# Relation sums kept per tile in a circular accumulator and projected per block of 512 nodes, with a group's one-hots made by two broadcast operations

## The chip, the cores and the metric

The kernel runs on one core of a Trainium2 chip. The metric is the device time of one launch in microseconds (us), as the median of repeated executions. A separate execution was recorded by the hardware profiler; the durations of single instructions come from it.

Engine names in the profile: PE is TensorE's matmul stream and PEld its weight loads, DVE is VectorE, ACT ScalarE, POOL GpSimd, SP SyncE. "L445" is line 445 of the kernel. The clock column of a profile, where there is one, is the clock granted to TensorE as a share of full speed.

## The reference

A graph with 12500 nodes of 128 features and 200000 edges, sorted by destination, goes through two relational convolutions, and the result is added to the input and normalized. The relation of an edge is the argmax over ten of its 42 attributes.

```python
def _rgcn_layer(x, src, dst, edge_type, w_rel, root, bias):
    N = x.shape[0]
    seg = dst * NUM_REL + edge_type
    xs = x[src]
    sums = jax.ops.segment_sum(xs, seg, num_segments=N * NUM_REL)
    cnt = jax.ops.segment_sum(jnp.ones(seg.shape, x.dtype), seg, num_segments=N * NUM_REL)
    mean = (sums / jnp.maximum(cnt, 1.0)[:, None]).reshape(N, NUM_REL, -1)
    return jnp.einsum('nrd,rdo->no', mean, w_rel) + x @ root + bias

edge_type = jnp.argmax(msg[:, NODE_EMB_DIM:-NODE_EMB_DIM], axis=1).astype(jnp.int32)
h = jax.nn.relu(_rgcn_layer(x, src, dst, edge_type, w_rel1, root1, b1))
y = _rgcn_layer(h, src, dst, edge_type, w_rel2, root2, b2)
return _layernorm(x + y, axis=-1)
```

All of it is f32. The destinations are sorted, so 128 neighbouring edges reach a narrow window of nodes.

## The kernel before

**Tiles and groups.** The edges are cut into 1563 tiles of 128. Sixteen tiles make a group; 97 such groups, one of eight tiles and one of three make the 99 groups of a layer. A tile's edges are taken to reach at most 12 consecutive nodes (`WN`), counted from its first node, so a pair (relation, node) is one of 10 x 12 = 120 keys (`KW`). If the data breaks this, a flag selects a slower general path at the end; with this data it is not entered.

**Per group** (`sums`, `project`, `add`):

1. POOL issues one indirect DMA for each tile (L445, `gather`), which brings the 128 source rows, 512 bytes each, into `g[:, j, :]`. `g` has three group buffers (`RING = 3`), so POOL can be up to three groups ahead of what frees them.
2. DVE makes a one-hot matrix for each tile, `oh[:, j, :]` (L461): 128 edges x 120 keys, equal to the edge's weight `wE` where the key `keyE` matches and 0 elsewhere. The weight is one over the count of edges with the same destination and relation. Two more operations make `at` (L465), which says where each of 96 rows, 8 tiles x 12 nodes, lies in a window of 160 nodes.
3. PE multiplies g by the one-hot (L468), sixteen times, into `zp`: per tile, the sum for each key, features on the partitions. `zp` has one buffer of four PSUM banks. Except in the last two groups the sums run from the last tile to the first, and the first of them waits for all gathers of the group.
4. ACT copies `zp` to `zs` (L482, four copies), sorted by relation.
5. PE projects: for each half of the group, ten matmuls with `w` of the ten relations (L494), accumulated in PSUM as `pp`; ACT copies it to `ms` (L500); PE multiplies `ms` by `at` (L510), which adds up rows of the same node.
6. DVE adds the 160 columns to `acc` (L516), features x all nodes, at the group's first node. That address is read from a table `bt` at run time, four at a time.

An f32 matmul shows up as two MATMUL rows in the profile, which I call two passes.

**Per block of 512 nodes** (29 blocks; the last ones have 128 and 84 nodes), once the groups that can reach it are done (`done_after`): `block_in` loads the rows of x (and in layer 1 of the hidden state from `hD` in DRAM) and transposes them on PE (L386), with an ACT copy to `fT` (L388). `block_rows` adds the bias to the accumulator on DVE (L395), clears it in layer 0 (L397), and on PE adds the root product (L400) and the transposed accumulator (L401). `hidden` applies the relu on ACT and stores to `hD`; `final` adds x, normalizes (L426 to L436) and stores the output.

**Once, spread over layer 0** in chunks of 128 tiles: `types` (the argmax, L266 to L271, and the keys) and `count` (equal keys within 40 neighbours, L341 to L350, which gives the weights). The first two chunks of types and the first of count run ahead of layer 0. Layer 1 starts its gathers from `hD` once layer 0 has stored all of it.

**Order.** The kernel is written in program order with the projection of one group after the sums of the next. The order on each engine is made by a scheduler at build time, and tile pools set the waits for buffers; a few instructions are pinned to program order (`keep_in_program_order`). Each engine executes its own list in order. All gathers stand in POOL's list; SP issues most of the other DMAs, ACT those of the weights and of `bt`.

Of the kernel before, what the change touches and what calls it, by code (L numbers as in the profile page):

```python
# [9 lines left out]
F32 = mybir.dt.float32  # L10
# [19 lines left out]
HR = HT * WN  # L30
SW = 160
# [4 lines left out]
YB = 512  # L36
W = 128
# [6 lines left out]
def rgcn_resnorm_kernel(ctx: ExitStack, tc: tile.TileContext, x, src, dst, attr, w_rel1, root1, b1,  # L44
# [26 lines left out]
    NPAD = N + SW  # L71
# [15 lines left out]
    assert C == P and E % GT == 0 and 0 < HALF < P and NT % CT and groups[-1][1] > 1  # L87
# [5 lines left out]
    ps_f = ctx.enter_context(tc.tile_pool(name="ps_f", bufs=2, space=PSUM))  # L93
    ps_c = ctx.enter_context(tc.tile_pool(name="ps_c", bufs=1, space=PSUM))

    hD = dram.tile([N, C], F32, name="hD")
    KD = dram.tile([1, L + NT * P + L], F32, name="KD")
# [8 lines left out]
    zpool = fast.enter_context(tc.tile_pool(name="zpool", bufs=2))  # L106
    spool = fast.enter_context(tc.tile_pool(name="spool", bufs=3))
    ps_z = fast.enter_context(tc.tile_pool(name="ps_z", bufs=1, space=PSUM))
    ps_o = fast.enter_context(tc.tile_pool(name="ps_o", bufs=1, space=PSUM))
# [47 lines left out]
    def sources(c):  # L157
# [9 lines left out]
    columns = const.tile([P, SW], F32, name="columns")  # L167
    nc.gpsimd.iota(columns, pattern=[[1, SW]], base=0, channel_multiplier=0,
                   allow_small_or_imprecise_dtypes=True)
    iota = columns[:, :W]  # L170
    pads = const.tile([P, L + 1], I32, name="pads")
    nc.gpsimd.iota(pads, pattern=[[1, L + 1]], base=FAR, channel_multiplier=0)

    rank = const.tile([G, 2 * HR], F32, name="rank")
    nc.gpsimd.memset(rank, 1.0)
    nc.gpsimd.affine_select(rank, rank, pattern=[[1, 2 * HR]], compare_op=ALU.is_ge, fill=0.0, base=0,
                            channel_multiplier=-WN)
    nc.gpsimd.affine_select(rank, rank, pattern=[[-1, 2 * HR]], compare_op=ALU.is_ge, fill=0.0, base=WN - 1,
                            channel_multiplier=WN)
    lead = const.tile([G, 2 * HR], F32, name="lead")  # L180
    nc.gpsimd.memset(lead, 1.0)
    nc.gpsimd.affine_select(lead, lead, pattern=[[0, 2 * HR]], compare_op=ALU.is_equal, fill=0.0, base=0,
                            channel_multiplier=1)
    which = const.tile([G, 1], F32, name="which")
    nc.gpsimd.iota(which, pattern=[[0, 1]], base=0, channel_multiplier=WN, allow_small_or_imprecise_dtypes=True)
    row = const.tile([HR, 1], F32, name="row")
    nc.gpsimd.iota(row, pattern=[[0, 1]], base=0, channel_multiplier=1, allow_small_or_imprecise_dtypes=True)
    lane = const.tile([P, P], F32, name="lane")
    nc.gpsimd.iota(lane, pattern=[[1, P]], base=0, channel_multiplier=P,
                   allow_small_or_imprecise_dtypes=True)  # L190
    riota = const.tile([P, NREL], F32, name="riota")
# [3 lines left out]
    iotaP = bank[:, :SW]  # L195
    riotaP = bank[:, SW:SW + NREL]
    topP = [bank[:, (3 + k) * P // 2:(4 + k) * P // 2] for k in range(2)]
    nc.vector.tensor_copy(iotaP, columns)
# [11 lines left out]
    within = const.tile([HR, 1], F32, name="within")  # L210
    pw = ps_f.tile([P, YB], F32, name="pf")
    nc.tensor.matmul(pw[:HR, 0:1], rank[:, :HR], which, start=True, stop=True)
    nc.vector.tensor_tensor(within, row, pw[:HR, 0:1], op=ALU.subtract)
    nc.vector.tensor_tensor(rank, rank, lead, op=ALU.subtract)
    fl = const.tile([P, 1], F32, name="fl")
    nc.vector.memset(fl, 0.0)
    acc = const.tile([P, NPAD], F32, name="acc")
    negs = const.tile([1, L], F32, name="negs")
# [5 lines left out]
    bt = keep.tile([1, NG], I32, name="bt")  # L224
    b8_i = keep.tile([G, NG], I32, name="b8_i")
    full = NT // G
    nc.vector.memset(b8_i[:, full:], 0)
    nc.scalar.dma_start(bt[:, :full + 1], bass.AP(dst.tensor, dst.offset, [[1, 1], [G * P, full + 1]]))
    nc.scalar.dma_start(b8_i[:, :full], bass.AP(dst.tensor, dst.offset, [[P, G], [G * P, full]]))
    for k, (t, n) in list(enumerate(groups))[full:]:  # L230
        if k > full:
            nc.scalar.dma_start(bt[:, k:k + 1], bass.AP(dst.tensor, dst.offset + t * P, [[1, 1], [1, 1]]))
        m = n if t + n < NT else n - 1
        nc.scalar.dma_start(b8_i[:m, k:k + 1], bass.AP(dst.tensor, dst.offset + t * P, [[P, m], [1, 1]]))
    nc.scalar.dma_start(b8_i[m:n, NG - 1:], bass.AP(dst.tensor, dst.offset + E - P, [[1, 1], [1, 1]]))
    b8 = keep.tile([G, NG], F32, name="b8")
    place = keep.tile([HR, 2, NG], F32, name="place")
    wide = const.tile([P, 1], F32, name="wide")
    nc.vector.memset(wide, 0.0)

    def places():
        early(0, nc.vector.tensor_scalar(bt, bt, 0, N - 1, op0=ALU.max, op1=ALU.min))
        early(0, nc.vector.tensor_copy(b8, b8_i))
        pw = ps_f.tile([P, YB], F32, name="pf")
        for h in range(2):
            nc.tensor.matmul(pw[:HR, h * NG:(h + 1) * NG], rank[:, h * HR:(h + 1) * HR], b8, start=True, stop=True)
        nc.vector.tensor_scalar(place, pw[:HR, :2 * NG].rearrange("p (h g) -> p h g", h=2), within, None, op0=ALU.add)
        nc.vector.tensor_reduce(wide[:HR], place, axis=AX.XY, op=ALU.max)
# [123 lines left out]

    def block_in(k, l):

        n0, n, subs = block(k)
        last = "e" if k == NBLK - 1 else ""
        b = len(subs) if last else 4
        xb = fin.tile([P, b, C], F32, name="xb" + last)
        rows_dma(xb, x, k, False)
        fb = xb  # L380
        if l:
            fb = fin.tile([P, b, C], F32, name="hb" + last)
            rows_dma(fb, hD, k, False)
        pt = ps_f.tile([P, YB], F32, name="pf")
        for t, h in subs:
            nc.tensor.transpose(pt[:, t * P:t * P + h], fb[:h, t, :], ident[:h, :h])  # L386
        fT = fin.tile([P, b * P], F32, name="fT" + last)
        nc.scalar.activation(fT[:, :n], pt[:, :n], AF.Copy)  # L388
        return xb, fT

    def block_rows(fT, k, l):

        n0, n, subs = block(k)
        a = fin.tile([P, YB], F32, name="a")
        nc.vector.tensor_scalar(a[:, :n], acc[:, n0:n0 + n], bsb[l], None, op0=ALU.add)  # L395
        if l == 0:
            nc.vector.memset(acc[:, n0:n0 + n], 0.0)  # L397
        pr = ps_f.tile([P, 4, C], F32, name="pf")
        for t, h in subs:
            nc.tensor.matmul(pr[:h, t, :], fT[:, t * P:t * P + h], rsb[l], start=True, stop=False)  # L400
            nc.tensor.matmul(pr[:h, t, :], a[:, t * P:t * P + h], ident, start=False, stop=True)  # L401
        return pr
# [5 lines left out]
    def hidden(k, ready):  # L408

        xb, fT = ready  # L410
        pr = block_rows(fT, k, 0)
        hb = fin.tile([P, 4, C], F32, name="hb")
        for p, s in spans(k):
            nc.scalar.activation(hb[:p, s], pr[:p, s], AF.Relu)
        rows_dma(hb, hD, k, True)

    def final(k, ready):

        xb, fT = ready
        pr = block_rows(fT, k, 1)  # L420
# [30 lines left out]
    def halves(n):  # L451
        return [(h, min(HT, n - h * HT)) for h in range(-(-n // HT))]
# [320 lines left out]
```

## Time and profile before

| what | value |
|---|---|
| median of three timed executions | 3974.79 us (3973.82 to 3981.2) |
| the profiled execution | 4772.34 us, of it the span from first to last instruction 4770.4 |
| granted TensorE clock, mean over the span | 0.739 |
| gathers | 3126, 944 ns each |
| first gather; last of layer 0 ends; first of layer 1; last ends | 4.30; 2390.5; 2422.18; 4732.4 us |

The profiled execution is 20% longer than the timed ones. A difference of this size means that its stalls can't simply be carried over; its durations of single instructions can.

Rows that stand around the change, as line, engine, operation, output<-inputs, count, then busy time, mean ns of one, and the idle time in front with what ended it:

```profile
L468 PE MATMUL zp<-oh,g 128*128 128x120 f32 x6252 | 1033.5, 325 | 293.5 <-issue 259.9
L482 ACT ACTIVATE zs<-zp 128x480 f32<-128x480 f32 (+1 forms) x782 | 382.9, 575 | 2167.7 <-remote 1912.9
L510 PE MATMUL pp<-at,ms 96*128 96x160 f32 (+1 forms) x784 | 198.1, 386 | 591.1 <-issue 405.0
L500 ACT ACTIVATE ms<-pp 96x256 f32<-96x256 f32 x196 | 74.1, 378 | 1241.3 <-remote 861.3
L465 DVE TENSOR_SCALAR at<-bank,place 96x160 f32<-96x160 f32 x392 | 131.9, 376 | 0.0
L426 DVE TENSOR_TENSOR v<-pf,xb 128x512 f32<-128x512 f32 (+1 forms) x28 | 17.4, 620 | 243.2 <-remote 238.3
```

"Issue" is time in which an engine waited for nothing that the profile shows; "remote" is a wait whose releaser could not be named.

### The profile page before, as it was taken

What the parts mean: (1) busy time and instruction counts of PE and PEld (TensorE: products, weight loads), DVE (VectorE), ACT (ScalarE), POOL (GpSimd) and SP (SyncE); (2) the same over time, 40 slices, a digit from 0 to 9 for tenths busy, and PEclk for the clock granted to TensorE, in tenths of its full rate; (3) what the DMA queues carried; (4) which work ended last, traced back from release to release, by engine and by line L of the source; (5) the groups of instructions that cost most, each with busy time, mean ns of one, the idle gap of its engine ahead of it and who ended that gap; (6) DMA issues with size and microseconds to landing.
All of it is one profiled execution on the core that took longest, in us unless ns stands there. A gap on an engine that the chain in (4) does not pass through costs nothing.

```text
span 4770.4 us, 43637 instructions
## 1 busy us (share of the span) xinstructions
PE 2759.5 (58%) x16162; PEld 2520.6 (53%) x16162; DVE 1511.5 (32%) x4652; ACT 527.0 (11%) x1136; POOL 2955.2 (62%) x3142
## 2 busy tenths in 40 slices
PE   2455556555655555666645555666655656565656
PEld 1455555555554545555544555555555555555556
DVE  5233333333333333333222222222222223222323
ACT  1011111111111101111110111111111111111111
POOL 5666665666656666666546666666666666666663
PEclk9677777777777777777776777777777777777778
DMA  4122122122221221212111211221222222222211
GB/s 141 44 79 74 50 74 74 50 75 62 61 77 47 75 62 51 57 48 52 46 49 46 54 52 51 53 56 51 52 56 53 52 52 58 51 52 52 58 52 40
DMA packets 180554, 279.00 MB, mean 58 GB/s; under 512 B 55623, under 2 KB 127190, under 8 KB 177206
## 3 DMA queue, kind: packets, MB, share of 16 engines
q0 software_dynamic: 100032, 205.07, 16.9%
q1 hardware_dynamic: 75428, 69.58, 4.6%
q8 instruction: 132, 2.16, 0.2%
q10 hardware_dynamic: 4872, 1.45, 0.1%
q14 instruction: 90, 0.74, 0.1%
HBM read 262.28 MB, written 13.60 MB: 58 GB/s over the span
## 4 chain that ended last, share of the span: by engine, by line
another core or an unknown queue 34%; PE 33%; issue 21%; DVE 11%; ACT 1%; DMA 0%; DVEq 0%; ACTq 0%; SPq 0%
PE pp L494 16%; PE zp L468 11%; DVE oh L461 7%; PE pp L510 2%; PE pf L401 1%; PE pf L400 1%; DVE at L465 1%; ACT zs L482 1%; DVE acc L516 1%; PE pf L343 0%; PE pf L345 0%; PE pf L386 0%; DVE o L436 0%; DVE st L429 0%
## 5 line engine op out<-in xcount | busy, mean ns | idle before, releaser
L445 POOL DMA_INDIRECT g<-in_x_dram,idxE x1563 | 1475.9, 944 | 911.2 <-issue 445.8
L445 POOL DMA_INDIRECT g<-hD,idxE x1563 | 1476.6, 945 | 865.3 <-issue 455.6
L494 PE MATMUL pp<-w,zs 128*96 128x128 f32 x7840 | 1358.2, 336 | 860.4 <-issue 722.1
L494 PEld LDWEIGHTS pp<-w,zs 128*96 128x96 f32 x7840 | 1232.0, 212 | 982.9 <-issue 834.6
L461 DVE TENSOR_SCALAR oh<-bank,keyE,wE 128x120 f32<-128x120 f32 x3126 | 1000.1, 400 | 644.6 <-remote 576.6
L468 PE MATMUL zp<-oh,g 128*128 128x120 f32 x6252 | 1033.5, 325 | 293.5 <-issue 259.9
L468 PEld LDWEIGHTS zp<-oh,g 128*128 128x128 f32 x6252 | 983.1, 240 | 314.0 <-issue 292.5
L482 ACT ACTIVATE zs<-zp 128x480 f32<-128x480 f32 (+1 forms) x782 | 382.9, 575 | 2167.7 <-remote 1912.9
L516 DVE TENSOR_TENSOR acc<-acc,pp 128x160 f32 x198 | 63.7, 322 | 1634.4 <-remote 1043.0
L510 PE MATMUL pp<-at,ms 96*128 96x160 f32 (+1 forms) x784 | 198.1, 386 | 591.1 <-issue 405.0
L510 PEld LDWEIGHTS pp<-at,ms 96*128 96x128 f32 (+1 forms) x784 | 142.5, 232 | 633.8 <-issue 437.1
L500 ACT ACTIVATE ms<-pp 96x256 f32<-96x256 f32 x196 | 74.1, 378 | 1241.3 <-remote 861.3
L341 DVE TENSOR_TENSOR eqb<-pf,kh 128x1344 bf16<-128x1344 f32 (+1 forms) x65 | 100.6, 1552 | 181.4 <-PE pf L345 82.3
L400 PE MATMUL pf<-root,fT 128*128 128x128 f32 x388 | 110.1, 379 | 79.0 <-issue 49.1
L401 PE MATMUL pf<-ident,a 128*128 128x128 f32 x392 | 114.0, 388 | 60.3 <-DVE a L395 22.0
L400 PEld LDWEIGHTS pf<-root,fT 128*128 128x128 f32 x388 | 87.0, 276 | 91.2 <-issue 55.8
L465 DVE TENSOR_SCALAR at<-bank,place 96x160 f32<-96x160 f32 x392 | 131.9, 376 | 0.0
L401 PEld LDWEIGHTS pf<-ident,a 128*128 128x128 f32 x392 | 90.7, 285 | 68.6 <-issue 24.6
L426 DVE TENSOR_TENSOR v<-pf,xb 128x512 f32<-128x512 f32 (+1 forms) x28 | 17.4, 620 | 243.2 <-remote 238.3
L348 DVE TENSOR_REDUCE wp<-pf 128x128 f32<-128x512 f32 (+1 forms) x13 | 9.0, 691 | 182.9 <-remote 175.5
L343 PE MATMUL pf<-eqb,identb 128*128 128x512 bf16 (+1 forms) x130 | 50.5, 388 | 17.9 <-DVE f L320 17.0
L388 ACT ACTIVATE fT<-pf 128x512 f32<-128x512 f32 (+1 forms) x56 | 30.2, 539 | 207.1 <-remote 151.3
(107 smaller groups left out, 483.0 us busy)
## 6 DMA issues: line engine op xcount, KB each, us to landing
m<-in_edge_attr_dram SPq DMA_DIRECT2D x24, 1344.0 KB
g<-in_x_dram,idxE POOLq DMA_INDIRECT x1563
g<-hD,idxE POOLq DMA_INDIRECT x1563
xb<-in_x_dram SPq DMA_DIRECT2D x46, 256.0 KB
hD<-hb SPq DMA_DIRECT2D x23, 256.0 KB
hb<-hD SPq DMA_DIRECT2D x23, 256.0 KB
out_dram<-o SPq DMA_DIRECT2D x23, 256.0 KB
w<-in_L_gnn_w_rel_dram ACTq DMA_DIRECT2D x2, 640.0 KB
```

What stands on the lines that cost most here:

```text
L341: nc.vector.tensor_tensor(eq[:p], kp[:p, None, :R].to_broadcast([p, DB, R]), ahead, op=ALU.is_equal)
L400: nc.tensor.matmul(pr[:h, t, :], fT[:, t * P:t * P + h], rsb[l], start=True, stop=False)
L401: nc.tensor.matmul(pr[:h, t, :], a[:, t * P:t * P + h], ident, start=False, stop=True)
L445: return g, [then("POOL", nc.gpsimd.indirect_dma_start(out=g[:, j, :], out_offset=None, in_=table, in_offset=bass.IndirectOffsetOnAxis(ap= ...
L461: then("DVE", nc.vector.tensor_scalar(oh[:, j, :], iotaP[:, :KW], keyE[:, t:t + 1], wE[:, t:t + 1], op0=ALU.is_equal, op1=ALU.mult))
L465: nc.vector.tensor_scalar(at[:, h, :], iotaP[:HR], place[:, h, k:k + 1], None, op0=ALU.is_equal)
L468: m = nc.tensor.matmul(zp[:, j // QB, j % QB * KW:(j % QB + 1) * KW], g[:, j, :], oh[:, j, :], start=True, stop=True)
L482: then("ACT", nc.scalar.activation(zs[:, :, b * QB:b * QB + m, :], zp[:, b, :m * KW].rearrange("c (j r n) -> c r j n", r=NREL, n=WN), AF.C ...
L494: nc.tensor.matmul(po[:m * WN, h], zs[:, r, h * HT:h * HT + m].rearrange("c j n -> c (j n)"), wsb[l][:, r, :], start=(r == 0), stop=(r == ...
L500: nc.scalar.activation(ms[:, :n // HT], po[:HR, :n // HT], AF.Copy)
L510: nc.tensor.matmul(pa, ms[:m * WN, h], at[:m * WN, h], start=(h == 0), stop=(h == len(parts) - 1))
L516: nc.vector.tensor_tensor(acc[:, s], acc[:, s], pa, op=ALU.add)
```

## The change

1. **Accumulators.** `acc` no longer holds projected features of all nodes. It is used as `circle`: features x 10 relations x (1024 + 12) nodes, a ring of nodes. For each tile, DVE adds the 10 x 12 sums of `zp` straight into `circle` at the tile's first node modulo 1024. So there are 16 additions at run-time addresses per group, with one load of 16 offsets, in place of one addition with a load for every four groups. An extra 12 columns at the end take what crosses the seam; every 1024 nodes they are added to the front and cleared.
2. **Projection.** `zs`, `project`, `ms`, `at` and the matmul with `at` are gone. Once per block, `projected` multiplies ten slices of `circle` by `w`, 512 columns at a time, on top of the root product, and ACT clears the slices. `zp` is now two tiles of eight, in two buffers, so a group's second half is still freed apart from its first.
3. **Block end.** ACT adds the bias and, in layer 0, applies the relu; PE transposes the result back. In layer 0 the untransposed result is stored as well (`hT`), and layer 1 loads it in place of the rows of `hD` and four transposes.
4. **One-hots.** Two operations per group over 128 x 16 x 120: equality of the column number with the key, both broadcast, and multiplication by the weight, which ACT has copied to PSUM.
5. **Set-up.** The tables for `at` are gone from POOL, PE and DVE. A table of every tile's first node replaces that of every group's: a DMA of 1562 single values, and on DVE seven operations on one row of 1563 (cast, difference from an even spread, two clamps, sum, modulo, and a check in `flagged`).

The core of the diff:

```diff
-        for j in range(n):
-            t = t0 + j
-            then("DVE", nc.vector.tensor_scalar(oh[:, j, :], iotaP[:, :KW], keyE[:, t:t + 1], wE[:, t:t + 1],
-                                                op0=ALU.is_equal, op1=ALU.mult))
-        at = spool.tile([HR, 2, SW], F32, name="at")
-        for h, _ in halves(n):
-            nc.vector.tensor_scalar(at[:, h, :], iotaP[:HR], place[:, h, k:k + 1], None, op0=ALU.is_equal)
-        zp = ps_z.tile([P, G // QB, YB], F32, name="zp")
+        wP = weightP[k % 3][:, :n]
+        then("ACT", nc.scalar.activation(wP, wE[:, t0:t0 + n], AF.Copy))
+        then("DVE", nc.vector.tensor_tensor(oh[:, :n], iotaP[:, None, :KW].to_broadcast([P, n, KW]),
+                                            keyE[:, t0:t0 + n, None].to_broadcast([P, n, KW]), op=ALU.is_equal))
+        nc.vector.tensor_tensor(oh[:, :n], oh[:, :n], wP[:, :, None].to_broadcast([P, n, KW]), op=ALU.mult)
+        zp = [ps_z.tile([P, HT // QB, YB], F32, name="zp") for _ in range(0, n, HT)]
...
+    def add(k, zp):
+
+        t0, n = groups[k]
+        lo, hi = bounds(t0, n)
+        lo, hi = (lo % RN, hi % RN) if lo // RN == hi // RN else (0, RN - 1)
+        offs = nc.values_load_multi_w_load_instructions(
+            bt_i[0:1, t0:t0 + n], engines=[DVE], min_val=lo, max_val=hi,
+            skip_runtime_bounds_check_because="clamped to these nodes on the chip")[1]
+        for j in range(n):
+            s = circle[:, :, ds(offs[j], WN)]
+            z = tile_sums(zp, j).rearrange("c (r n) -> c r n", n=WN)
+            nc.vector.tensor_tensor(s, s, z, op=ALU.add)
...
+    def projected(fT, k, l):
+
+        n0, n, subs = block(k)
+        po = ps_p.tile([P, YB], F32, name="pp")
+        nc.tensor.matmul(po[:, :n], rsb[l], fT[:, :n], start=True, stop=False)
+        o = n0 % RN
+        if not o and k:
+            nc.vector.tensor_tensor(circle[:, :, :WN], circle[:, :, :WN], circle[:, :, RN:], op=ALU.add)
+            nc.scalar.activation(circle[:, :, RN:], zero[:, None, :WN].to_broadcast([P, NREL, WN]), AF.Copy)
+        H = NREL // 2
+        for q in range(0, NREL, H):
+            for r in range(q, q + H):
+                nc.tensor.matmul(po[:, :n], wsb[l][:, r, :], circle[:, r, o:o + n], start=False, stop=(r == NREL - 1))
+            nc.scalar.activation(circle[:, q:q + H, o:o + n], zero[:, None, :n].to_broadcast([P, H, n]), AF.Copy)
+        return po
...
     def places():
-        early(0, nc.vector.tensor_scalar(bt, bt, 0, N - 1, op0=ALU.max, op1=ALU.min))
-        early(0, nc.vector.tensor_copy(b8, b8_i))
...
+        early(0, nc.vector.tensor_copy(bt, bt_i))
+        early(0, nc.vector.tensor_tensor(off, bt, even, op=ALU.subtract))
+        early(0, nc.vector.tensor_scalar(bt_i, off, float(OFF), -float(OFF), op0=ALU.min, op1=ALU.max))
+        early(0, nc.vector.tensor_tensor(bt_i, bt_i, even, op=ALU.add))
+        early(0, nc.vector.tensor_scalar(bt_i, bt_i, 0, N - 1, op0=ALU.max, op1=ALU.min))
+        early(0, nc.vector.tensor_scalar(bt_i, bt_i, RN - 1, None, op0=ALU.bitwise_and))
...
-        nc.vector.tensor_scalar(a[:, :n], acc[:, n0:n0 + n], bsb[l], None, op0=ALU.add)
...
+        nc.scalar.activation(a[:, :n], po[:, :n], AF.Identity if l else AF.Relu, bias=bsb[l])
         pr = ps_f.tile([P, 4, C], F32, name="pf")
         for t, h in subs:
-            nc.tensor.matmul(pr[:h, t, :], fT[:, t * P:t * P + h], rsb[l], start=True, stop=False)
-            nc.tensor.matmul(pr[:h, t, :], a[:, t * P:t * P + h], ident, start=False, stop=True)
+            nc.tensor.transpose(pr[:h, t, :], a[:, t * P:t * P + h], ident)
...
-        pr = block_rows(fT, k, 0)
+        n0, n, _ = block(k)
+        a, pr = block_rows(sums_of(fT, k, 0), k, 0)
+        then("SP", nc.sync.dma_start(hT[:, n0:n0 + n], a[:, :n]))
```

In the program that results, each of the 16 additions waits for the one before it; the second of a group's two one-hot operations stands between additions of an older group; the first eight sums of a group wait for the first eight additions of the group before, the last eight for the last eight.

## The prediction

> **What bounds the kernel now.** I read the share of busy time first, then the costliest groups, then the waits of POOL, then its timeline.
>
> ```profile
> PE 2759.5 (58%) x16162; PEld 2520.6 (53%) x16162; DVE 1511.5 (32%) x4652; ACT 527.0 (11%) x1136; POOL 2955.2 (62%) x3142
> L445 POOL DMA_INDIRECT g<-in_x_dram,idxE x1563 | 1475.9, 944 | 911.2 <-issue 445.8
> L445 POOL DMA_INDIRECT g<-hD,idxE x1563 | 1476.6, 945 | 865.3 <-issue 455.6
> L494 PE MATMUL pp<-w,zs 128*96 128x128 f32 x7840 | 1358.2, 336 | 860.4 <-issue 722.1
> L461 DVE TENSOR_SCALAR oh<-bank,keyE,wE 128x120 f32<-128x120 f32 x3126 | 1000.1, 400 | 644.6 <-remote 576.6
> L341 DVE TENSOR_TENSOR eqb<-pf,kh 128x1344 bf16<-128x1344 f32 (+1 forms) x65 | 100.6, 1552 | 181.4 <-PE pf L345 82.3
> L516 DVE TENSOR_TENSOR acc<-acc,pp 128x160 f32 x198 | 63.7, 322 | 1634.4 <-remote 1043.0
> ```
>
> No engine is full. POOL is the fullest, and nearly all of it is one instruction, the gather of 128 rows. Now what POOL waited for, and one group of it:
>
> ```profile
> POOL g L445 <- issue: 901.4, 2925, 5.1
> POOL g L445 <- remote: 456.6, 129, 8.1
> POOL g L445 <- PE zp L468: 383.2, 61, 28.5
> POOL g L445 <- DMA hD<-hb: 31.7, 1, 31.7
> ```
>
> ```profile
> 1420.64 0.94 POOL L445 DMA_INDIRECT g<-in_x_dram,idxE  x1 [0.30 <-issue]
> 1425.12 0.94 POOL L445 DMA_INDIRECT g<-in_x_dram,idxE  x1 [3.55 <-remote]
> 1426.37 0.94 POOL L445 DMA_INDIRECT g<-in_x_dram,idxE  x1 [0.30 <-issue]
> ...
> 1443.84 0.95 POOL L445 DMA_INDIRECT g<-in_x_dram,idxE  x1 [0.30 <-issue]
> 1448.40 0.94 POOL L445 DMA_INDIRECT g<-in_x_dram,idxE  x1 [3.61 <-PE zp L468]
> ```
>
> Inside a group gathers start every 1.249 us (1425.12, 1426.37). That is 0.94 of work and 0.30 of "issue", which recurs before nearly every gather, so it is part of the gather's price. A group of 16 takes 19.98 us. Then POOL waits some 3.6 us, because the ring of three group buffers is full and the sums of an older group (L468) are late. So the recorded execution is bound by PE, at about 23.3 us per group.
>
> The timed runs are not. The recorded execution took 4772.3 us, the timed ones 3974.8. I split the recorded span: first gather at 4.3; 3126 x 1.249 = 3904 of gathers; 825 of larger gaps, of which 28.2 lie in the head (63.2 to 92.7), 31.4 at the layer boundary and some 766 in the ring stalls of single groups; 38 after the last gather. Sum 4771. The timed median has room for 4 + 3904 and some 66 more. Head, boundary and tail as recorded are 98. But two of these hold PE's backlog:
>
> ```profile
> 4738.07 4.53 PE L494 MATMUL pp<-w,zs 128*96 128x128 f32 x40
> ...
> 4755.11 0.60 PE L468 MATMUL zp<-oh,g 128*128 128x120 f32 x4
> ```
>
> The last gather ended at 4732.4, yet the last sums ran at 4755.1, behind the projections of older groups. At the boundary the distance is the same, 22.4 us (2390.5 to 2412.9). Without a backlog it would be about 6, so 16 go twice: 98 - 32 = 66. Hence the timed kernel is **bound by POOL issuing gathers**, with next to no ring stalls. The "issue" gaps of 1 to 2 us between single matmuls belong to the recording. What the change can move in the timed runs is head, boundary and tail (66 us), unless it makes another engine need more than 20 us per group.
>
> **The change part by part.**
>
> *PE.* Gone per group: the 40 passes of L494, four of L510. Per block come a root matmul and ten w·circle matmuls of 512 columns. The trace has no f32 matmul of this width; its 512-column bf16 pass takes 0.215 warm and 0.427 cold, so 11 x 2 passes are about 5 to 10 us each block if a pass is alike, doubled if an f32 pass takes two of those; I take 10. PE falls from 13 to 15 us busy per group to about 4 to 7, plus 10 per four groups. In the timed runs this is worth nothing: gathers hide it. In a recorded run it removes the 766.
>
> *DVE one-hots.* Sixteen of L461 start 0.31 apart (5.05 us) and two of L465 take 0.7. In their place stand two operations over 1920 elements. Nearest row: L341, 1344 elements in 1.552; scaled by element 2.15 each, 4.3 together. The ends are 1.9 and 2.5 each. Saving 1.4 per group, hidden.
>
> *DVE adds.* One L516 (0.32) becomes 16 dynamic adds of 120 elements, each waiting for the one before it, with a register operation each and one load of 16 offsets. L516 has 160 elements, so 0.28 to 0.32; a dependent operation starts 0.04 after its predecessor ends; the register operation (0.069) runs beside the predecessor in L516's rows. Spacing 0.32 to 0.36: 5.1 to 5.8 us, plus 0.4 to 0.8 for the load (a load of four takes 0.34, on a busy engine 0.79). Upper end: the register operation and its wait don't overlap, 0.5 each, 8 us. I take 5.3 + 0.6: no row shows a reason for the gap.
>
> *The new wait.* Two halves of PSUM hold one group: the first eight sums of group k+1 wait for adds 0 to 7 of k, the last eight for adds 8 to 15. Behind the waiting matmul stand all later PE work, and for its end wait the adds of k+1 and the gathers of k+4. Chain per group: DVE 4.3 + 5.9 = 10.2, the sums' second half 1.8, hops 0.3: **12.3 us, against 19.98 for the gathers**.
>
> Here a rule speaks against the change. The Trainium skill, "TensorE: Matmul & The Clock Gate", Part 1 (HAM clock gate): after an idle window of about 3.4 us TensorE falls to half its clock and needs as long busy to recover. A PE with 5 us of work in 20 would then be cold most of the time. The trace has both speeds: a pass of L468 takes 0.112 warm, 0.213 cold, and the granted clock is 0.739 on average. By the warm row the second half (16 passes) is 1.8, by the rule 3.4, so the chain is 12.3 or 13.9; the block's matmuls take up to 18 instead of 10. Both stay below the cover: four groups have 80 us, and even 4 x 13.9, 8 more of projection between two sums, 7 of DVE at a block of layer 1 (L426 to L436) come to 71. In layer 0 the types and count steps add about 9 of DVE per four groups (five L341 per eight groups make half of it): 73. The ring holds more than 30 us of lag for uneven groups. Cost 0; if the cover goes, the excess over 80 is paid 50 times.
>
> *ACT.* Four zs copies and ms (2.3 us per group) go; weight copy, zeroing (two of 2560 elements, about 2.4 each from the 512-column fill of 0.61), a and hb come. A weight copy may queue behind a zeroing that waits for the projection, so one-hots can be some 6 us late once a block. Hidden by the ring.
>
> *POOL, SP, DMA.* POOL loses about 1.4 us of head set-up that stands behind the first gathers. SP gets one store of hT per block of layer 0 ahead of hD's, and one load in place of hb's in layer 1; both far ahead of use, except at the boundary (below). Gathers beside L395 averaged 0.974 against 0.944; L395 goes: 58 x 0.03 = -2 us.
>
> *Head.* Seven operations on one row of 1563 come before the first argmax: 1.0 to 1.8 each, 9 to 12 us; about 5 of it falls where DVE waited for a DMA (14.9 to 20.3). That is +4 to +7 on the chain to the first weights, wE at 80.5, and so on the 28.2 us for which POOL stands. Given back: the first L341 now follows two small operations instead of some ten slow self-waiting ones (57 to 66.9), up to -10; one-hots -0.7. From -7 to +8; I take 0, since both lie on the same chain.
>
> *Boundary and tail.* The last sums to the first gather of layer 1 took 9.25 (2412.93 to 2422.18). Gone: 20 passes of L494 (2.1), ms, L510 and one add (1.4). Come: three adds (1.0), the last block's 11 matmuls of 84 columns (2 to 2.5), zeroing before it (1.4), bias, transpose instead of L400/L401 (+0.5), hT's store ahead of hD's. +1.5 +-3, twice: +3.
>
> Sum: 0 - 2 + 0 + 3 = +1. On the recorded execution: 4772 - 766 - 32 of backlog + 1 = 3975; on the median of the timed runs, 3975 + 1 = **3976 us**. Its own range, from head and boundary, is 3962 to 3990. A measurement here tells 0.2% (8 us) from no change.
>
> **The rivals.**
>
> *DVE becomes the bound (slower; 0.17).* Place: adds in layer 0. Price: the upper end above, 0.5 an add instead of 0.33, adds 2.7 per group, so with a cold TensorE four groups take 73 + 11 = 84 in layer 0 and 82 in layer 1 against 80: 25 x 4 + 25 x 2 = 150 more, 4126. It decides from about 0.44 per add (7 us spread over 64 adds). For it: self-waiting small operations in the head show gaps of 1.3 to 2.6 us. Against: those have "issue" and "remote" as their cause, and operations of 0.82 in the argmax start 0.86 apart.
>
> *Before was held by more than gathers (faster; 0.20).* If the gather is cheaper unrecorded than 1.249, before was partly bound by PE, and the change frees it: at 1.22, 3126 x 0.029 = 91 less, 3885; or only some 15 us of ring stalls remain in the timed runs, 3960. For it: the split of 66 us rests on my estimate of the backlog. Against: the sum closes at 1.249 within 2 us.
>
> *Head decides (slower; 0.08).* Nothing of the +8 is given back and the boundary takes +6 more: 3990.
>
> *Nothing hidden changes (0.55)*, the forecast: of it 0.25 within 0.2%, 0.16 faster by the head's gain, 0.14 slower.
>
> Together: faster 0.36, same 0.25, slower 0.39. The range for 8 in 10 takes in part of both tails: 3915 to 4060.
>
> **What would show it.** In the changed kernel's profile: a span near 3975, gathers 1.249 apart through whole groups with few gaps above 0.30; 16 adds in 5 to 6 us; the two one-hot operations near 2.15; PE under 35% busy with a low granted clock; POOL's stall in the head between 20 and 36. Wrong if POOL waits in most groups for sums, and those for adds, or if the gap between gathers itself differs.

## The result, and the profile after

The changed kernel takes **3992.68 us** (median of five executions, 3991.27 to 3994.05). Five executions of the kernel before, taken beside it, have a median of 3973.87 (3973.28 to 3981.2). The ratio is 1.0047 with a 95% interval of 1.0036 to 1.0057: the change makes the kernel 18.8 us slower, a small loss that is clear of the noise.

In every recording of the kernel before and in all experiment runs each kernel took some 16 to 20% longer than in the runs above, because PE's matmuls or its signals came late (the last section), so those runs are compared only among themselves. The recording of the changed kernel is free of this: it is one of the five executions, with a time of 3992.68, a span of 3990.8 and a mean clock of 0.704.

First the rows of the page of the changed kernel that answer to those shown of before: busy time and share of each engine, then groups of instructions with busy time, mean ns of one, and idle time in front.

```profile
PE 1771.3 (44%) x8122; PEld 1419.5 (36%) x8122; DVE 1946.0 (49%) x4394; ACT 357.8 (9%) x523; POOL 2957.3 (74%) x3136
L451 POOL DMA_INDIRECT g<-in_x_dram,idxE x1563 | 1479.5, 947 | 496.5 <-issue 469.0
L451 POOL DMA_INDIRECT g<-hD,idxE x1563 | 1475.2, 944 | 501.5 <-issue 471.5
L495 DVE TENSOR_TENSOR acc<-acc,zp 128x120 f32 x3126 | 863.8, 276 | 1506.8 <-PE zp L472 1371.7
L386 PE MATMUL pp<-acc,w 128*128 128x512 f32 (+2 forms) x1160 | 437.0, 533 | 11.7 <-DVE acc L495 7.0
L467 DVE TENSOR_TENSOR oh<-bank,keyE 128x1920 f32<-128x1920 f32 (+1 forms) x198 | 419.8, 2120 | 25.9 <-PE zp L472 25.0
L469 DVE TENSOR_TENSOR oh<-oh,bank 128x1920 f32<-128x1920 f32 (+1 forms) x198 | 419.6, 2119 | 0.2
```

The engine that gained work is DVE (32% before, 49% now). It waits 1372 us for sums, so it is not short of time. POOL's waits say the same from the other side (total, number, longest):

```profile
POOL g L451 <- issue: 940.5, 3086, 0.3
POOL g L451 <- DMA hD<-hb: 25.4, 1, 25.4
POOL g L451 <- PE zp L472: 20.1, 3, 17.5
```

The "issue" gaps are never longer than 0.3: gathers start 1.250 us apart, group after group, and of 3125 gaps only four are larger. They are 17.5 us in the head, 1.7, 0.9, and 25.4 at the layer boundary. So the ring never runs full in mid-layer. The span is 4.5 to the first gather, 3126 gathers at 1.250 (3907), 44 more for the four gaps, and 35 after the last gather. So the changed kernel can have lost 18.8 us in three places only: head, boundary and tail.

### The profile page after: what moved, and what is told of

Same layout as the page of the kernel before. It is cut to its first block, busy times and chain, and to the rows that moved or that the text cites. A ratio compares the mean times of both kernels' runs of the same rounds, so it can differ in the third digit from the quotient of the medians.

```text
span 3990.8 us, 29921 instructions
## 1 busy us (share of the span) xinstructions
PE 1771.3 (44%) x8122; PEld 1419.5 (36%) x8122; DVE 1946.0 (49%) x4394; ACT 357.8 (9%) x523; POOL 2957.3 (74%) x3136
## 5 line engine op out<-in xcount | busy, mean ns | idle before, releaser
L472 PE MATMUL zp<-oh,g 128*128 128x120 f32 x6252 | 1178.8, 373 | 2004.4 <-DMA g<-hD,idxE 996.7
L472 PEld LDWEIGHTS zp<-oh,g 128*128 128x128 f32 x6252 | 1143.1, 286 | 2099.9 <-issue 2081.0
L495 DVE TENSOR_TENSOR acc<-acc,zp 128x120 f32 x3126 | 863.8, 276 | 1506.8 <-PE zp L472 1371.7
L386 PE MATMUL pp<-acc,w 128*128 128x512 f32 (+2 forms) x1160 | 437.0, 533 | 11.7 <-DVE acc L495 7.0
L467 DVE TENSOR_TENSOR oh<-bank,keyE 128x1920 f32<-128x1920 f32 (+1 forms) x198 | 419.8, 2120 | 25.9 <-PE zp L472 25.0
L469 DVE TENSOR_TENSOR oh<-oh,bank 128x1920 f32<-128x1920 f32 (+1 forms) x198 | 419.6, 2119 | 0.2
L387 ACT ACTIVATE acc<-zero 128x2560 f32<-128x2560 f32 (+2 forms) x116 | 231.9, 2000 | 939.2 <-PE pp L386 939.2
L386 PEld LDWEIGHTS pp<-acc,w 128*128 128x128 f32 x1160 | 203.9, 196 | 210.6 <-issue 198.0
L405 PE MATMUL pf<-ident,a 128*128 128x128 f32 x196 | 34.7, 297 | 16.4 <-ACT a L402 16.3
L405 PEld LDWEIGHTS pf<-ident,a 128*128 128x128 f32 x196 | 26.3, 157 | 19.7 <-ACT a L402 19.7
```

The source lines that it names most:

```text
L386: nc.tensor.matmul(po[:, :n], wsb[l][:, r, :], circle[:, r, o:o + n], start=False, stop=(r == NREL - 1))
L387: nc.scalar.activation(circle[:, q:q + H, o:o + n], zero[:, None, :n].to_broadcast([P, H, n]), AF.Copy)
L405: nc.tensor.transpose(pr[:h, t, :], a[:, t * P:t * P + h], ident)
L467: then("DVE", nc.vector.tensor_tensor(oh[:, :n], iotaP[:, None, :KW].to_broadcast([P, n, KW]), keyE[:, t0:t0 + n, None].to_broadcast([P, n ...
L469: nc.vector.tensor_tensor(oh[:, :n], oh[:, :n], wP[:, :, None].to_broadcast([P, n, KW]), op=ALU.mult)
L472: m = nc.tensor.matmul(tile_sums(zp, j), g[:, j, :], oh[:, j, :], start=True, stop=True)
```

## Where the last groups wait

The timeline of PE in the tail of the changed kernel (start, duration, line, matmul, count, and idle time in front with what ended it). The last gather ended at 3955.85.

```profile
3949.48 2.40 PE L386 MATMUL pp<-acc,w 128*128 128x128 f32 x20
...
3958.14 4.05 PE L386 MATMUL pp<-acc,w 128*128 128x128 f32 x20 [4.62 <-DVE acc L495]
...
3967.90 4.48 PE L472 MATMUL zp<-oh,g 128*128 128x120 f32 x22 [4.08 <-DVE oh L469]
3974.21 3.87 PE L386 MATMUL pp<-acc,w 128*128 128x128 f32 x20 [1.83 <-DVE acc L495]
...
3980.06 2.46 PE L386 MATMUL pp<-acc,w 128*128 128x84 f32 x20 [0.38 <-DVE acc L495]
```

The sums of the last two groups (L472, 22 passes) start 12 us after the last gather. They wait for their one-hots, and DVE's timeline shows why these are late:

```profile
3964.29 0.18 DVE L436 BATCH_NORM_AGGREGATE mv<-st 128x2 f32<-128x6 f32 x1
3964.84 0.16 DVE L439 RECIPROCAL rstd<-rstd 128x1 f32<-128x1 f32 x1 [0.36 <-ACT rstd L438]
3965.04 0.34 DVE L442 TENSOR_SCALAR o<-v,mv,rstd 128x128 f32<-128x128 f32 x1
3965.45 1.16 DVE L467 TENSOR_TENSOR oh<-bank,keyE 128x960 f32<-128x960 f32 x1
...
3978.89 0.59 DVE L495 TENSOR_TENSOR acc<-acc,zp 128x120 f32 x2 [4.73 <-ACT acc L387]
```

The one-hots stand behind the normalization of a block, which waited for that block's projection. Later, the additions of the last three tiles (3978.89) wait 4.73 us for ACT to clear the slices (L387) of a block that is being projected. And two of the projections run cold: 20 passes of 128 columns took 2.40 at 3949.48, where the granted clock was 1.00, but 4.05 and 3.87 here, after PE had stood idle, where it was 0.59 and 0.61.

At the boundary PE shows the same chain. The last gather of layer 0 ended at 1979.2.

```profile
1979.60 2.50 PE L472 MATMUL zp<-oh,g 128*128 128x120 f32 x12
1986.80 4.63 PE L386 MATMUL pp<-acc,w 128*128 128x128 f32 x20 [4.69 <-DVE late L565]
1991.22 1.17 PE L472 MATMUL zp<-oh,g 128*128 128x120 f32 x6
```

The last sums (x6) run behind a projection, which is slow as well (4.63, at a granted clock of 0.50). That projection waited for additions: the one before it ended at 1986.74, just ahead of the operation on L565 that the row names. The trace of DVE has 4.3 us of one-hots (L467 at 1982.14, L469 at 1984.41) among these additions, and they are those of layer 1's first group, which nobody needs for another 40 us.

Of the kernel before there is no recording without the late signals, so its three places are known only in sum. Its time of 3973.87 is a span of about 3972.0. In the changed kernel everything from the 49th gather to the last, without the boundary, takes 3844.6. If before takes the same there, which means no ring stalls and the same spacing (none of its recordings can show it), that leaves 127.4 for the start of the 49th gather (the first after the stall in the head) plus boundary plus tail. In the changed kernel these are 85.8 + 25.4 + 35.0 = 146.2. The difference is the 18.8, by subtraction.

## The experiments

In each kernel the two ends after the last gathers were read: boundary (last gather of layer 0 to first of layer 1) and tail (last gather to the end). These stretches hold the backlog that a kernel brings along: in the changed kernel the two are 89.0 here and 60.4 in the undisturbed recording. So it is differences between kernels that are read, not the lengths. The runs were made on three chips; ratios are to the kernel before on the same chip, with 95% intervals.

```
kernel        time     ratio, interval            49th gather  ring stalls  boundary  tail
before_again  4768.64  (one run)                     92.3         756         31.7    38.0
before_3      4771.55  (one run)                     92.2         759         31.8    37.8
before_4      4767.78  (one run)                     91.6         748         31.7    38.0
after_again   4644.83  0.9763, 0.9741 to 0.9785      85.5         603         39.0    49.9
end_oh        4650.42  0.9759, 0.9745 to 0.9772      87.8         623         36.5    42.5
end_both      4645.98  0.9769, 0.9754 to 0.9783      87.7         613         34.3    42.0
ends          4639.06  0.9746, 0.9732 to 0.9759      87.4         626         33.0    37.2
ends_again    4639.94  0.9756, 0.9736 to 0.9775      88.0         625         33.0    35.8
ends_head     4653.22  0.9777, 0.9764 to 0.9791      91.5         630         33.1    35.8
places_late   4661.10  0.9787, 0.9773 to 0.98        95.6         626         39.2    51.3
oh_x2         4739.71  0.9950, 0.9935 to 0.9966      91.1         692         51.6    51.3
oh_single     4638.16  0.9756, 0.9737 to 0.9775      87.4         599         39.1    49.9
```

"Ring stalls" is the sum of POOL's gaps after the first 96 gathers beyond 0.3 each, without the boundary; they fall from some 755 to 603 with the change, which is most of why it is 2.4% faster in these runs and 0.5% slower where gathers run through.

**The two kernels again** (no edit).

> The unchanged kernel of before, profiled once more, to get an execution whose ring stalls are not those of the first recording. Theory A (the change loses at the two ends of a layer): if the recording is undisturbed (span near 3972), gathers stand 1.249 to 1.250 apart, POOL's stall in the head is 20 to 28 us, its wait at the layer boundary about 15 and the tail after the last gather 20 to 25, against 20, 25 and 35 in the changed kernel. Theory B (the head decides): head stall at most 5, boundary 25, tail 35. Theory C (gathers were cheaper before): spacing 1.244 or less.

> The changed kernel itself, beside before on the same chip. In the first four runs every kernel, before too, took about 4650 to 4770 us, and in their traces TensorE's signals reached the waiting engines only when POOL's gathers had stopped. If this chip does the same, I expect about 4660 against 4763 for before, a ratio near 0.98: one stop of some 2.6 us per group instead of 3.2 and more. If it does not, 3992 against 3974.

> The unchanged kernel of before, for a recording in which gathers run through. If it is one: theory A (the change loses at the ends of the layers): head stall 20 to 28 us, boundary wait about 15, tail 20 to 25, against 20, 25 and 35. Theory B (the head decides): head stall at most 5, boundary 25, tail 35. Theory C (gathers were cheaper before): spacing 1.244 or less.

> The unchanged kernel of before, for a recording in which gathers run through. Theory A: POOL stands at 80 to 92 us for its 49th gather; boundary wait plus tail 34 to 46, against 60 in the changed kernel. Where signals are held up: 92, and 70 for boundary and tail, as recorded twice.

None of the three recordings of before was undisturbed, so the values that theories A to C forecast for such a recording were not tested. The one line of POOL's waits that stands for the boundary, first of the kernel before (before_3), then of the changed kernel (after_again):

```profile
POOL g L445 <- DMA hD<-hb: 31.8, 1, 31.8
```

```profile
POOL g L451 <- DMA hD<-hb: 39.0, 1, 39.0
```

Boundary and tail together are 69.7, 69.6 and 69.7 in three recordings of before and 89.0 in the changed kernel: **19.3 us more, where 18.8 were lost**. The boundary has 4.0 more until the last sums end and 3.3 after them; the tail has 6.9 more until the last sums end and 5.1 after. Only the part until the last sums holds the backlog. In the changed kernel it is 26.5 and 30.2 here, against 13.2 and 16.5 undisturbed; what follows is 12.5 and 19.7, against 12.2 and 18.4. From the cold projection on, the tail repeats the waits of the undisturbed recording (PE of after_again):

```profile
4612.85 3.93 PE L386 MATMUL pp<-acc,w 128*128 128x128 f32 x20 [4.63 <-DVE acc L495]
...
4622.49 4.42 PE L472 MATMUL zp<-oh,g 128*128 128x120 f32 x22 [4.08 <-DVE oh L469]
4628.80 3.99 PE L386 MATMUL pp<-acc,w 128*128 128x128 f32 x20 [1.89 <-DVE acc L495]
...
4634.77 3.14 PE L386 MATMUL pp<-acc,w 128*128 128x84 f32 x20 [0.38 <-DVE acc L495]
```

So what comes after the last sums carries over to the timed runs of the changed kernel, and in before it takes 9.25 and 14.6. The 11 us until the last sums are a difference between two backlogs, and less sure for the timed runs.

**end_oh: the last two groups' one-hots ahead of the last additions.** They get tiles of their own and come before the blocks that end with those additions.

```diff
+            if k == NG - 2:
+                for e in (k, k + 1):
+                    early_oh[e] = one_hots(e)
             if end:
                 while held:
```

> The changed kernel, with the one-hots of the last two groups of a layer written ahead of the last full group's additions. Theory A: in the tail the sums of the group of eight no longer start at 3967.9 but as their gathers land, so the tail of 35.0 falls to about 25; the boundary, where these one-hots were early already, stays within 2 us: 3983 in all. Theories B and C: 3992, no change.

Boundary 36.5 and tail 42.5: 10 of the 19.3 are gone, 7.4 of them in the tail, where 10 were expected, and 2.5 at the boundary. The one-hots were late in the tail, as read above. The total didn't follow (ring stalls 623 against 603), so this run shows the place and not a gain.

**end_both: also, nothing of later use between the boundary's additions.** The first operations on the flag's tables go behind the last sums, and the first two one-hots of layer 1 behind layer 0's last addition.

```diff
+        if k < 2 and "add" in last:
+            tc.add_manual_dep(eq.ins, last["add"].ins.name, behind, reason="the last additions first")
...
+        for ins in first:
+            tc.add_manual_dep(ins.ins, last["sum"].ins.name, behind, reason="not at the boundary")
```

> The changed kernel with three things moved at the ends of the layers: the one-hots of the last two groups ahead of the last full group's additions, the first one-hots of layer 1 behind layer 0's last additions, and the flag's table work away from the boundary. Theory A, where gathers run through: tail 35.0 to about 25, boundary wait 25.4 to about 18, some 17 us in all: 3975, level with before. Theories B and C: 3992, no change. Where TensorE's signals are held up: about 10 us less than the changed kernel.

Boundary 34.3, another 2.2 less. That is half of the 4.3 us that the two one-hots take; the projection in front of the last sums stayed. The total did not fall by the 10 us that were expected: 4646 against 4645.

**ends, ends_again: also, the blocks that the last three groups complete wait for the last addition, and the last blocks of layer 1 are not cleared.** The clearing that is left out has no reader after it.

```diff
+        spent = l and done_after(k) > groups[NG - 3][0]
...
+            if spent:
+                continue
             nc.scalar.activation(circle[:, q:q + H, o:o + n], zero[:, None, :n].to_broadcast([P, H, n]), AF.Copy)
...
             add(k, zp)
+            if NG - 3 <= k < NG - 1:
+                return
```

> end_both, and the additions of the last three groups all ahead of the blocks that they complete: those three blocks are projected one after the other at the end, and layer 1 doesn't clear what it no longer reads. Theory A (the last groups' sums and the last blocks' projections stand in each other's way): tail of 42.0 in end_both to 33 or less, boundary wait of 34.3 to 30 or less, where TensorE's signals are held up; where gathers run through, tail 35.0 to about 22, boundary 25.4 to about 15, 3970 in all, below before. Rival (the ends are bound by what any order must do after the last gather): no more than 2 us.

> The kernel ends once more. Where gathers run through on this chip: 3970, against 3974 for before and 3992 for the changed kernel (theory A), or 3990 (the rival). Where signals are held up, 4639 as before, boundary and tail 33 and 37, which gives their scatter.

Boundary and tail come to 70.2 and 68.8, where before has 69.7. All of the 19.3 is taken back with the same sums, additions and projections: at the boundary by order alone (1.3 more than in before is left), in the tail by order and the clearings left out together (0.7 to 2.2 less than in before). Neither end came down to what was expected (a tail of 33 or less, a boundary of 30 or less). The tail of ends on PE, to be read against that of after_again (the last gather ended at 4611.6):

```profile
4619.23 2.40 PE L387 MATMUL pp<-acc,w 128*128 128x128 f32 x20
...
4625.43 5.02 PE L489 MATMUL zp<-oh,g 128*128 128x120 f32 x22 [2.16 <-DVE acc L513]
4630.24 3.03 PE L387 MATMUL pp<-acc,w 128*128 128x128 f32 x20
...
4635.07 2.50 PE L387 MATMUL pp<-acc,w 128*128 128x128 f32 x20 [0.73 <-DVE acc L513]
...
4638.43 2.40 PE L387 MATMUL pp<-acc,w 128*128 128x84 f32 x20
```

The idle times in front have shrunk, and with them the price of a projection after the last sums: 2.4 to 3.0 where it was 3.1 to 4.0. In the total time ends and ends_again are 5 to 6 us below the changed kernel, with intervals of the ratios that overlap, and their ring stalls are some 20 longer. So these runs don't show a faster kernel. Where gathers run through, 3992.7 less 19 to 20 would be about 3973, level with before; that is an estimate, and it was not measured.

**places_late and ends_head: the seven operations on one row of 1563 later.** In places_late they follow the first count (on the changed kernel), in ends_head they stand between types and count (on ends).

```diff
-    places()
     for _ in chain(types(0), types(1)):
         pass
     for _ in count(0):
         pass
+    places()
```

> The changed kernel, with the table of first nodes computed after the head's types and count. Theory A: wE some 5 us earlier, sums delayed by the two table operations that now stand beside the one-hots, POOL's head stall 17.6 to about 13: 3988. Theory B: most of the loss goes, 3978 or less.

> ends, with the table of first nodes computed between the types of the first two chunks and the first count, where the changed kernel's VectorE waits 5.7 us for a load. Theory A, by its steps (seven operations cost 4 to 7 us ahead of the first argmax): the keys of the second chunk at about 47 instead of 54, POOL's stall in the head 17 to about 12. Rival (places_late: the head is not bound by them): the stall stays at 17 or grows, because the small operations wait for each other as they did there.

Both missed: the 49th gather came later (95.6 and 91.5 against 85.5 and 87.4), not earlier. What the seven operations pushed back did come forward, the second chunk's first key (L289) from 54.1 in after_again to 45.2 in places_late. But then a chain of small operations fell in front of the count's first equality. DVE's timeline of places_late:

```profile
51.93 0.15 DVE L302 TENSOR_SCALAR f<-f 128x1 f32<-128x1 f32 x1 [1.80 <-remote]
54.03 0.29 DVE L300 TENSOR_REDUCE f<-bad 128x1 f32<-128x128 f32 x1 [1.95 <-remote]
...
57.53 0.16 DVE L304 TENSOR_TENSOR fl<-fl,f 128x1 f32<-128x1 f32 x1 [1.93 <-issue]
...
61.03 0.29 DVE L289 TENSOR_SCALAR key<-d_f 128x128 f32<-128x128 f32 x1 [3.18 <-issue]
```

Some operations of 0.15 to 0.3 us start 2 to 3.5 us after the one before, as they do in the recordings of before (57.05, 59.15, 61.95); in the changed kernel such operations stand 0.1 to 0.35 apart in both of its recordings (40.07 to 40.90 undisturbed). Why is open. So the runs say that the order in the head matters more than the seven operations, but not what the head of before costs where signals aren't late.

**oh_x2: two more equality operations per group**, which write the same values again, 4.3 us of DVE per group.

```diff
+        for _ in range(2):
+            nc.vector.tensor_tensor(oh[:, :n], iotaP[:, None, :KW].to_broadcast([P, n, KW]),
+                                    keyE[:, t0:t0 + n, None].to_broadcast([P, n, KW]), op=ALU.is_equal)
```

> The changed kernel, with two more equality operations over 1920 elements per group, 4.3 us more of DVE per group. Theory A, with a chain of 12.3 to 14 us per group under a cover of 19.98: gathers stay 1.25 apart in the middle of both layers; some 4 us more in the head and a few at the boundary: about 4000. Rival (DVE is already close to deciding): 2 us or more per group, over 4250.

It is 95 us slower than the changed kernel (89 by the ratios, as the two ran on different chips), some 0.48 per group for 4.3 of added work. If DVE were close to being the bound, each group would have paid 2 us and more. In the recordings 89 more are ring stalls and 13 more lie at the boundary. A group in these runs takes about 23 us and not 20, so the cover is larger here than in the timed runs; for those, what shows that DVE isn't the bound is the changed kernel's own trace (no ring stalls).

**oh_single: the changed kernel with the sixteen one-hots of before** and no copy of the weights.

```diff
+        for j in range(n):
+            t = t0 + j
+            then("DVE", nc.vector.tensor_scalar(oh[:, j, :], iotaP[:, :KW], keyE[:, t:t + 1], wE[:, t:t + 1],
+                                                op0=ALU.is_equal, op1=ALU.mult))
```

> The changed kernel with one part of the change undone: sixteen one-hot operations per group as before, and no weight copy. Theory A (the one-hots are hidden, 5.05 us on VectorE against 4.3, and the gain and the loss come from the projection's part alone): within 10 us of the changed kernel where signals are held up (about 4645 to 4655), a boundary and tail of 39 and 50 as in the changed kernel. Rival (the broadcast one-hots are what moves the time): back toward 4760 where signals are held up; toward 3974 where gathers run through.

Ends of 89.0, as in the changed kernel, and nearly the same time (4638 and 4645, ratios of 0.9756 and 0.9763 with intervals that overlap). The broadcast one-hots are no part of the loss.

## Why the prediction was right, and where it was not

Forecast 3976, measured 3992.7: inside the range of 3915 to 4060, just outside the likeliest case's own range of 3962 to 3990, and slower, to which 0.39 was given. The range was kept wide for the rivals; the sum itself gave +1 where +18.8 was measured.

- **The bound is POOL's gathers: right.** In the changed kernel no ring stalls are left, and head, boundary and tail are the only places that matter.
- **The recorded execution of before is bound by PE, and the change removes the 766: wrong in mechanism.** PE was held up there and stood still in 949 us of short pauses; its work was not the limit (the last section). With the change PE has 1771 us busy where it had 2760, or 1821 in after_again, and there 603 of some 755 us of ring stalls are still left.
- **PE's relief worth nothing in the timed runs: right, as far as the total shows.** PE is 44% busy, not under 35%. The block's ten matmuls of 512 columns take 8.76 (10 was taken for eleven), the sixteen sums 6.1: 8.3 per group of 20 us, which is inside the prediction's own terms; the 35% didn't follow from them.
- **Cold or warm PE: nearer to the rule.** In mid-layer the granted clock was 0.67 to 0.75 (four stretches of 80 us). The second half of the sums was put at 1.8 by the warm row and at 3.4 by the rule of the Trainium skill, "TensorE: Matmul & The Clock Gate", Part 1, that TensorE falls to half its clock after an idle window of about 3.4 us. Half of 6.1 is 3.05. In mid-layer this is hidden, as the prediction said. Its price at the ends was not in the sum.
- **DVE: right.** One-hots 2.15 each for a full group (2.15 predicted), additions 0.276 long and 0.313 apart (0.32 to 0.36). The load of sixteen offsets takes 1.10 instead of 0.4 to 0.8, off the chain.
- **The new wait hidden by the ring: right.** The gathers that reuse a buffer start 32 us after the sums that free it (at the least 23, behind the first groups).
- **Head 0: not refuted.** The stall is 17.5, below the 20 to 36 that the prediction looked for; the stall of before where signals aren't late isn't known. If the ends lost 19.3 in the timed runs as they did in the recordings, the head lost 18.8 - 19.3 = -0.5. That is argued from a difference; if the 49th gather of before started at 92.2 in the timed runs too, the head gained 6 and the ends lost 25. For the changed kernel it starts alike in both kinds of recording (85.8 and 85.5). How the 18.8 divide between head and ends stays open.
- **Boundary and tail: the step that failed.** The term was "+1.5 +-3, twice: +3"; the recordings give +7.3 and +12.0. It counted the instructions that the last block gains and loses, which stand behind the last sums: +3.3 and +5.1 there. For the time until the last sums it put nothing, and took for granted that they end about 6 us after the last gather, an estimate for before that no run measured. They ended 13.2 and 16.5 us after it. Left out were the one-hots standing behind a block's normalization, the block projection in front of the last sums, the wait of 4.73 for a clearing, and projections at the cold price of 3.9 to 4.6 instead of 2.4. Putting these into another order (end_oh, end_both, and ends, which also leaves out clearings) took back 10, 12.7 and 18.8 to 20.2 of the 19.3. Hence the cause is shown in the length of the ends in the recordings. No run shows it clear of noise in the total time, and that it accounts for the same 18.8 in the timed runs rests on the equal size.
- **Rivals.** DVE as the bound (4126) fell with the trace. Before held by more than gathers forecast a gain (3885 or 3960), and the changed kernel, which has no ring stalls at all, is not faster; a few us of ring stalls in the timed runs of before, made up for by a larger loss at the ends, are not excluded. Head decides (3990) has the number nearest to the measured one, but that is luck: the 49th gather starts at 85.8, not later than the 92 of before's recordings, and the tail, where most was lost, had no part in it. Only its boundary (1.5 and 6 more) came near the measured +7.3.

## What to carry to other kernels

Where one engine sets the pace throughout, price a change where this engine stands still: start, stage boundary, end. There the instructions of the last items come onto the path, and their order on the other engines counts as much as their number: list what stands in each queue behind the last transfer, at the price of an engine that has been idle. Work that moves from "per group" to "per block" leaves the hidden middle and returns, undivided, at each end.

## What the hardware showed besides

**Signals of PE that arrive late.** Gathers start 1.25 us apart while POOL runs. In the recording of the changed kernel 485 of 532 signals of PE (after the first 100 us) register within 1.25 us of a gather's start, so while POOL runs. In the run after_again only 71 of 500 do, and 323 register 3 to 5 us after the last gather's start, once POOL has stopped. One case in end_oh, POOL and PE:

```profile
1069.41 0.95 POOL L451 DMA_INDIRECT g<-in_x_dram,idxE  x1 [0.30 <-issue]
1073.08 0.95 POOL L451 DMA_INDIRECT g<-in_x_dram,idxE  x1 [2.73 <-PE pp L386]
```

```profile
1056.79 6.49 PE L482 MATMUL zp<-oh,g 128*128 128x120 f32 x32 [16.68 <-issue]
1063.12 8.76 PE L386 MATMUL pp<-acc,w 128*128 128x512 f32 x20
```

The sums ended at 1063.3 and the projection at 1071.9, yet signals of both registered together at 1072.82 to 1073.04. POOL and DVE waited for sums that had been done for 9 us. DVE's own signals in mid-layer were not held (additions 0.31 apart in both kinds of recording). What holds PE's stays open.

In the recordings of before PE's matmuls are held as well. PE and then POOL, in the first of them:

```profile
1005.85 0.26 PE L468 MATMUL zp<-oh,g 128*128 128x120 f32 x1 [1.82 <-issue]
1007.98 0.36 PE L468 MATMUL zp<-oh,g 128*128 128x120 f32 x1 [1.86 <-issue]
1010.08 0.36 PE L468 MATMUL zp<-oh,g 128*128 128x120 f32 x1 [1.74 <-issue]
...
1013.76 0.94 POOL L445 DMA_INDIRECT g<-in_x_dram,idxE  x1 [6.05 <-PE zp L468]
```

PE makes 619 such pauses of 1 to 3 us there, 949 us in all, with nothing that the profile shows to wait for; in after_again it makes 21, in the undisturbed recording none. Half of PE's signals (381 of 766) register there while POOL runs. What causes the pauses stays open too.

**Operations on one partition stretch gathers.** POOL and DVE in the head of the changed kernel:

```profile
13.94 2.73 POOL L451 DMA_INDIRECT g<-in_x_dram,idxE  x1 [0.30 <-issue]
16.97 0.94 POOL L451 DMA_INDIRECT g<-in_x_dram,idxE  x1 [0.30 <-issue]
```

```profile
13.70 1.77 DVE L226 TENSOR_TENSOR off<-bt,even 1x1563 f32<-1x1563 f32 x1
```

A gather that started during this operation with two inputs in SBUF took 2.73 instead of 0.94; four others beside operations on the row of 1563 took 1.39 to 1.58, and one that started 0.18 ahead of such an operation took 0.94. The Trainium skill, "SBUF — State Buffer", section "Who interferes with whom", states that an operation with two inputs in SBUF contends with GpSimd's reads; the trace agrees, though it does not show which access of the gather is held. Some 4 us in all, hidden here, since POOL stood for 17.5 us in the head anyway.
